# A graph layer's sum tiles in PSUM: zeroed by TensorE instead of ScalarE, and counts with a one-column weight

## The chip, the cores and the metric

The kernel runs on one core of one Trainium2 chip, in one launch. A time is the device time of one execution in microseconds. The kernel before has a median of 3023.34 us over 12 runs (3010.74 to 3027.88).

## The reference, cut to what matters

Two relational graph convolutions and a mixture of experts, on 6250 nodes with 256 features, 100000 edges sorted by target, 8 relations:

```python
def _rgcn_conv(x, W, Wroot, b, src, dst, etype):
    xs = x[src]
    seg = dst * R + etype                                   # R = 8
    sums = jax.ops.segment_sum(xs, seg, num_segments=N * R)
    cnt = jax.ops.segment_sum(jnp.ones_like(xs[:, 0]), seg, num_segments=N * R)
    mean = (sums / jnp.maximum(cnt, 1.0)[:, None]).reshape(N, R, -1)
    return x @ Wroot + b + jnp.einsum('nrd,rde->ne', mean, W)

h = relu(_rgcn_conv(layernorm(x), W1, Wroot1, b1, src, dst, edge_type))
x = x + _rgcn_conv(h, W2, Wroot2, b2, src, dst, edge_type)
x = x + ffn(layernorm(x))      # 8 experts, the best 2 of each row, gelu between two products
```

The change lies in the two segment sums (`sums` and `cnt`).

## The kernel before, in words

The program has four stages. The first normalises `x` and writes it to HBM as three bf16 parts (`xs`), since the sums are made of bf16 products of three parts each. It also works out each edge's place, and sets `flag`: 1 if the edges lie where a plan expects them (every edge in its window, every window in its bounds). If it is 1, the two graph layers run as function `layer` (k = 0 and 1); otherwise a generic arm does that work, with an edge list sorted by indirect DMAs. The last stage runs the experts; the change does not touch it.

**Tiles and groups.** The edges come in 782 tiles of 128. One to six consecutive tiles form a group, 194 groups in a layer, and a group's edges fall into a window of at most 64 consecutive target nodes (`WIN`). `_plan` fixes the groups, their windows' widths (`regions[r][5]`, `wd` in the code), the order in which two runs of groups, one upward and one downward through the nodes, are taken in turns (`seq`), and `whole[b]`, the step by which every edge into the 128-node block b has been added. `bounds` lists for each group which blocks its window may touch.

**A step.** `layer` runs through 194 steps (q). `tiles_in` of the next group takes a PSUM tile `pg` (two buffers), lets ScalarE fill it with zeros (L672), and for each tile of edges issues an indirect gather on GpSimd's queue (L680, the tile `ge`, 13 buffers) and one VectorE instruction that makes the one-hot matrix `oh` (L686). `sums` of this step's group multiplies each gathered tile with its `oh` on TensorE: six bf16 matmuls for two halves of the features and three parts (L696), and in layer 0 a seventh with a matrix of ones for the counts (L699). All of them add onto the zeros in PSUM. `add` adds `pg` to a ring in SBUF on VectorE (L710).

**Blocks.** Around it, by `whole[b]`: `root` loads a block's rows a step ahead; `counts` and `invert` give 1/count; `project`, two steps after `whole[b]`, multiplies the block's sums with the nine weight matrices (36 f32 matmuls, L783) and collects them on VectorE (L791, L793); `clear` zeroes the block's part of the ring on ScalarE (L800); `finish` and `turn` write the result and transpose it. All engines take their instructions in order. The order within a step is `tiles_in` of the next group, `project` and `clear`, `turn`, `finish`, `sums`, `invert`, `add`, `root` and `counts`. Layer 1's gathers read what layer 0's `finish` wrote, so layer 1 begins after layer 0's last block.

Because the group's adds and the block's matmuls touch the same ring, the program declares by `bounds` which of them need no order between them; `READ` and `TAKE` are the numbers of steps that these declarations allow.

Of the kernel before, what the change touches and what calls it, by code (L numbers as in the profile page):

```python
# [39 lines left out]
BF16 = mybir.dt.bfloat16  # L40
# [8 lines left out]
P = 128  # L49
# [45 lines left out]
Z = 4.8  # L95
WIN = 64
RB = 3
READ = 2
TAKE = 3
EARLY = 30  # L100

# [1 line left out]
def _plan(N, E, R):  # L103

    T = -(-E // P)

    def windows(ts, n):

        mid = n // 2
        lo, hi = [0] * n, [-(1 << 30)] * n
        for t in ts:
            for k in range(n + 1):
                i0, i1 = t * P, max(0, t + k - mid) * P
                mean = N * (i1 * i1 - i0 * i0) / (E * E)
                sd = 2 * N * i0 / (E * E) * math.sqrt(abs(i1 - i0)) + 0.004 * abs(mean)
                if k < n:
                    lo[k] = min(lo[k] if t != ts[0] else 1 << 30, math.floor(mean - Z * sd) - (k < mid))
                if k:  # L120
                    hi[k - 1] = max(hi[k - 1], math.ceil(mean + Z * sd) + (1 if k <= mid else 2))
        shift = -min(lo)
        w = [(a + shift, b + shift) for a, b in zip(lo, hi)]
        return shift, w, max(b for _, b in w)


    NB = -(-N // P)
    mid = max(0, round((N / 4 - P / 2) / P))
    split = round(T * math.sqrt((mid + 0.5) * P / N))
    regions = []  # L130
    t = 0
    while t < T:
        left = (split if t < split else T) - t
        for n in range(min(6, left), 0, -1):
            ng = max(1, min(36, left) // n)
            shift, w, width = windows((t + n // 2, t + n * (ng - 1) + n // 2), n)
            if width <= WIN:
                break
        regions.append((t, n, ng, shift, w, width))
        t += n * ng  # L140
    groups = []
    for r, (t0, n, ng, *_) in enumerate(regions):
        for g in range(ng):
            groups.append((t0 + g * n, n, r))
    NG = len(groups)
    up = [g for g in range(NG) if groups[g][0] < split]
    down = list(range(NG - 1, len(up) - 1, -1))
    size = [sum(groups[g][1] for g in s) for s in (up, down)]
    seq, at, n = [], [0, 0], [0, 0]
    while len(seq) < NG:  # L150

        s = int(n[1] * (size[0] - EARLY) < n[0] * size[1])
        if at[s] == len((up, down)[s]):
            s = 1 - s
        g = (up, down)[s][at[s]]
        seq.append(g)
        at[s] += 1
        n[s] += groups[g][1]
    step = {g: q for q, g in enumerate(seq)}

    whole = []
    for b in range(NB):
        if b == mid:
            whole.append(NG - 1)
            continue
        p = math.sqrt((b + 1 if b < mid else b) * P / N)
        dev = Z * math.sqrt(E * p * (1 - p)) + 1
        t = int(min(E - 1, E * p + dev) // P) if b < mid else int((E * p - dev) // P)
        whole.append(step[next(g for g, (t0, n, _) in enumerate(groups) if t0 + n > t)])


    bounds = []
    for g in range(NG):
        read, taken = ([b for b in range(NB) if whole[b] + n < step[g]] for n in (READ - 1, TAKE))
        if g < len(up):
            bounds.append((sum(b < mid for b in read) or -NB, sum(b < mid for b in taken) + RB))
        else:
            n = sum(b > mid for b in read)
            bounds.append((NB - sum(b > mid for b in taken) - RB, NB - n if n else 2 * NB))
    return T, regions, groups, seq, len(up), mid, whole, bounds  # L180
# [3 lines left out]
def kernel(  # L184
# [20 lines left out]
    nc = tc.nc  # L205
    N, D = x.shape
    E = src.shape[0]
    R = gW1.shape[0]
    X = fW1.shape[0]
    H = fW1.shape[2]  # L210
    KD = D // P
    KH = H // P
    NB = -(-N // P)
# [20 lines left out]
    def rows(i):  # L234
        return P if i < NB - 1 else LAST
# [6 lines left out]
    ones16 = const.tile([P, P], BF16, name="ones16")  # L242
# [82 lines left out]


    T, regions, groups, seq, UP, mid, whole, bounds = _plan(N, E, R)
    assert T == C
    NG = len(groups)
# [306 lines left out]
    with tc.If(go == 1) as cmp:  # L636
        with ExitStack() as arm:
            TR = MM = 2
            TT = "mm"
            ap = arm.enter_context(tc.tile_pool(name="ap", bufs=2, side="right"))  # L640
            invs = ap.tile([P, NB, R], F32, name="invs", bufs=1)
            hTs = ap.tile([P, NB, KD, P], F32, name="hTs", bufs=1)
            zeros = ap.tile([P, WIN], F32, name="zeros", bufs=1)
            nc.vector.memset(zeros, 0.0)
            rings = [ap.tile([P, KD + 1, R, RING + WIN], F32, name=f"ring{i}", bufs=1) for i in range(2)]

            step = {g: q for q, g in enumerate(seq)}
# [8 lines left out]
            def layer(k):  # L656
                nd = KD + 1 if k == 0 else KD
# [8 lines left out]
                state = {}  # L666

                def tiles_in(g):
                    t0, n, r = groups[g]
                    pg = psum.tile([P, nd, R, WIN], F32, name="pg", tag="pg", bufs=2)  # L670
                    wd = regions[r][5]
                    state["zeroed"] = nc.scalar.copy(pg[:, :nd, :, :wd],  # L672
                                                     zeros[:, None, None, :wd].to_broadcast([P, nd, R, wd]))
                    got = []
                    ohs = ap.tile([P, OHW], BF16, name="oh", bufs=3)
                    o0 = 0
                    for t in range(t0, t0 + n):
                        m = P if t < EC else ER
                        ge = ap.tile([P, 3, KD, P], BF16, name="ge", bufs=13)
                        nc.gpsimd.indirect_dma_start(  # L680
                            out=ge[:m].rearrange("p s k d -> p (s k d)"), out_offset=None, in_=xs[k][:, :],
                            in_offset=bass.IndirectOffsetOnAxis(ap=idx[:m, t : t + 1], axis=0))
                        a, b = regions[r][4][t - t0]
                        oh = ohs[:m, o0 : o0 + (b - a) * R].rearrange("p (r d) -> p r d", r=R)
                        o0 += (b - a) * R
                        nc.vector.tensor_scalar(oh, iota16[:m].rearrange("p (r d) -> p r d", r=R)[:, :, a:b],  # L686
                                                rel[:m, t : t + 1], None, op0=OP.is_equal)
                        got.append((ge, oh, m, a, b))
                    state[g] = (pg, got)

                def sums(g):
                    pg, got = state[g]
                    for ge, oh, m, a, b in got:
                        for c in range(KD):
                            for s in range(3):
                                nc.tensor.matmul(pg[:, c, :, a:b], ge[:m, s, c, :], oh, start=False, stop=False,  # L696
                                                 skip_group_check=True)
                        if nd > KD:
                            nc.tensor.matmul(pg[:, KD, :, a:b], ones16[:m], oh, start=False, stop=False,  # L699
                                             skip_group_check=True)  # L700

                def add(g):
# [132 lines left out]
                def logits(b):  # L835
                    if k == 1:
                        gate(place[b], state.pop(("t", b)), rows(b))
                        for o, bs in batches[:-1]:
                            if b == bs[-1]:
# [3 lines left out]
                                todo.extend((j, i, False, c) for j, i in enumerate(bs))  # L843

                tiles_in(seq[0])
                due = {}
                for b, q in enumerate(whole):
# [45 lines left out]
    with cmp.Else():  # L893
        with ExitStack() as arm:
# [35 lines left out]
            with tc.tile_pool(name="sortp", bufs=1, side="right") as sp:  # L930
# [22 lines left out]
                for d in range(NB):  # L953
                    oh = sp.tile([P, C], F32, name="oh", bufs=2)
# [16 lines left out]
                for d in range(NB):  # L971
                    oh = sp.tile([P, C], F32, name="oh", bufs=2)
# [11 lines left out]
                for j in range(C):  # L984
                    n = P if j < EC else ER
# [11 lines left out]
                for i in range(NB):  # L997
                    n = rows(i)
# [13 lines left out]
                for j in range(C):  # L1012
                    a = sp.tile([P, P], F16, name="ca", bufs=4)
                    nc.vector.tensor_scalar(a, iota_k[:, :P], df[:, j : j + 1], None, op0=OP.is_equal)
                    b = sp.tile([P, NK], F16, name="cb", bufs=4)
# [7 lines left out]
            ap = lay.enter_context(tc.tile_pool(name="aggp", bufs=2, side="right"))  # L1023
# [65 lines left out]
            for i in range(NB):  # L1089
                n = rows(i)  # L1090
# [10 lines left out]
            with tc.tile_pool(name="ggate", bufs=2) as gp, tc.If(go == 0):  # L1101
                for o, bs in batches:
                    for j, i in enumerate(bs):
                        n = rows(i)
# [5 lines left out]
                    if i != order[-1]:  # L1110
                        c = choose(bs, o, gp, "mm", MM)
# [162 lines left out]
```

## Time and profile before

| | |
|---|---|
| median of 12 runs | 3023.34 us |
| the profiled execution | 3020.25 us, of which its span is 3018.4 us |
| busy over the span | TensorE matmul 2557.0 us, weight loads 2158.7, GpSimd 1808.6, VectorE 1621.7, ScalarE 1018.8 |
| gathers of edges (L680) | 1564, 1519.7 us, the first at 83.8 and the last at 2153.4 us |
| sums (L696) and counts (L699) | 9384 and 782 matmuls, 837.4 and 189.0 us |
| block products (L783, from the ring) | 3072 matmuls of 128x256 f32, 727.2 us |
| zeroing of `pg` (L672) | 388 copies on ScalarE, 380.1 us |
| adding to the ring (L710) | 388 on VectorE, 456.5 us |

In the profile an instruction is named by its line, its engine and the tile that it writes and reads (`pg<-oh,ge`). PE is TensorE's matmul, PEld its weight load, DVE is VectorE, ACT ScalarE, POOL GpSimd. What stands behind an arrow `<-` after an idle time is what ended that idle time. A matmul's busy time includes the end of its pipeline, so a busy engine can still start matmuls closer together.

### The profile page before, as it was taken

To read this page: it belongs to the slowest core of one execution; us is meant where nothing else is said; L and a number is where in the kernel's file an instruction comes from. 1 tells how busy PE (TensorE), PEld (TensorE's weight loads), DVE (VectorE), ACT (ScalarE), POOL (GpSimd) and SP (SyncE) were. 2 spreads that over 40 slices of the span, in tenths; PEclk is the share of its full clock that TensorE was granted. 3 is DMA by queue.
4 is the path that set the end of the run, shared out by engine and by line. 5 is a ranking of instruction groups with operands and counts; after the bars stand their busy time and mean duration, and the time that the engine had idled before them with its cause. 6 is when DMAs were issued, how large, how long until landed. Compare 5 with 4: busy or idle time off the path is not lost.

```text
span 3018.4 us, 52037 instructions
## 1 busy us (share of the span) xinstructions
PE 2557.0 (85%) x18131; PEld 2158.7 (72%) x18131; DVE 1621.7 (54%) x4676; ACT 1018.8 (34%) x1378; POOL 1808.6 (60%) x2109
## 2 busy tenths in 40 slices
PE   5578887888888886887888888898839999999997
PEld 2467776776777765666766776777628888888886
DVE  7567676766676674666766776676711111111111
ACT  6434444434344342332323322232312222222221
POOL 1667777777777765777777777777413333333332
PEclk9689999999999997988989998899969999999999
DMA  7555565655565544666566666666363444444441
GB/s 248 157 151 164 168 172 165 172 158 169 161 174 165 166 140 140 178 176 174 170 173 176 173 176 172 173 183 174 108 200 114 116 111 107 108 122 107 107 121 20
DMA packets 215591, 461.05 MB, mean 153 GB/s; under 512 B 50716, under 2 KB 123222, under 8 KB 215190
## 3 DMA queue, kind: packets, MB, share of 16 engines
q0 software_dynamic: 120384, 334.45, 41.2%
q1 hardware_dynamic: 83724, 112.33, 11.1%
q10 hardware_dynamic: 11210, 10.81, 1.1%
q8 instruction: 149, 2.44, 0.3%
q14 instruction: 124, 1.02, 0.1%
HBM read 412.02 MB, written 46.31 MB: 152 GB/s over the span
## 4 chain that ended last, share of the span: by engine, by line
PE 63%; DMA 20%; ACT 5%; issue 5%; DVE 4%; POOL 2%; SPq 0%; DVEq 0%; ACTq 0%; POOLq 0%
PE pr L783 25%; DMA ge<-xs,idx 15%; PE ph L1214 12%; PE po L1225 12%; PE pg L696 10%; ACT ring L800 2%; DVE ring L710 2%; POOL ge L680 2%; DMA xt<-in_x_dram 2%; ACT pg L672 2%; DMA cn<-ring 1%; PE pt L1198 1%; PE pg L699 1%; DMA fw<-in_L_ffn_W_dram 1%; PE pt L314 1%
## 5 line engine op out<-in xcount | busy, mean ns | idle before, releaser
L680 POOL DMA_INDIRECT ge<-xs,idx x1564 | 1519.7, 972 | 617.1 <-issue 215.0
L696 PE MATMUL pg<-oh,ge 128*128 128x200 bf16 (+24 forms) x9384 | 837.4, 242 | 314.4 <-DMA ge<-xs,idx 220.7
L696 PEld LDWEIGHTS <-ge 128*128 128x128 bf16 x9384 | 675.5, 105 | 439.4 <-DMA ge<-xs,idx 280.3
L783 PE MATMUL pr<-gw,ring 128*128 128x256 f32 (+1 forms) x3136 | 744.1, 392 | 1.1 <-DVE h L793 0.6
L783 PEld LDWEIGHTS pr<-gw,ring 128*128 128x128 f32 (+1 forms) x3136 | 609.6, 197 | 95.3 <-DVE h L793 5.0
L710 DVE TENSOR_TENSOR ring<-pg,ring 128x1176 f32 (+31 forms) x388 | 456.5, 1176 | 285.8 <-PE pg L696 145.3
L672 ACT COPY pg<-zeros 128x1176 f32<-128x1176 f32 (+31 forms) x388 | 380.1, 981 | 543.8 <-DVE ring L710 500.3
L793 DVE SCALAR_TENSOR_TENSOR h<-pr,invs,h 128x256 f32<-128x256 f32 (+1 forms) x784 | 376.5, 480 | 159.3 <-PE pr L783 142.1
L800 ACT COPY ring<-zeros 128x3072 f32<-128x3072 f32 (+1 forms) x98 | 227.8, 2324 | 670.4 <-PE pr L783 610.3
L1215 ACT ACTIVATE hT<-ph,bcol 128x256 f32<-128x256 f32 x424 | 200.3, 473 | 535.9 <-PE ph L1214 535.9
L1214 PE MATMUL ph<-xT,w 128*128 128x256 f32 x1696 | 379.6, 383 | 0.0
L1225 PE MATMUL po<-fw,hT 128*128 x1696 | 374.4, 379 | 0.0
L1225 PEld LDWEIGHTS po<-fw,hT 128*128 128x128 f32 x1696 | 322.2, 190 | 43.8
L1214 PEld LDWEIGHTS ph<-xT,w 128*128 128x128 f32 x1696 | 322.0, 192 | 42.6
L686 DVE TENSOR_SCALAR oh<-iota,rel 128x152 bf16<-128x152 f16 (+25 forms) x1564 | 336.8, 274 | 19.0 <-PE pg L699 14.1
L1186 POOL DMA_INDIRECT xg<-xnd,ti x106 | 105.3, 994 | 348.9 <-DMA ti<-tlist 250.4
L1230 POOL DMA_INDIRECT out_dram<-fo,ti x106 | 168.6, 1591 | 231.5 <-DVE wt L1199 119.1
L1228 DVE TENSOR_TENSOR fo<-po,b2b 128x256 f32<-128x256 f32 x106 | 45.0, 424 | 299.5 <-PE po L1225 299.5
L699 PE MATMUL pg<-oh,ones 128*128 128x128 bf16 (+24 forms) x782 | 189.0, 242 | 0.0
L1209 DVE COPY bcol<-b1c 128x8 f32 x53 | 9.4, 179 | 302.1 <-ACT hT L1215 301.6
L699 PEld LDWEIGHTS <-ones 128*128 128x128 bf16 x782 | 83.0, 106 | 2.7
L783 PE MATMUL pr<-gw,hTs 128*128 128x256 f32 (+1 forms) x196 | 70.6, 483 | 2.3 <-ACT hTs L831 2.1
(190 smaller groups left out, 1344.9 us busy)
## 6 DMA issues: line engine op xcount, KB each, us to landing
w<-in_L_ffn_W_dram SPq DMA_DIRECT2D x53, 1024.0 KB
ge<-xs,idx POOLq DMA_INDIRECT x1564
xt<-in_x_dram SPq DMA_DIRECT2D x96, 128.0 KB
xs<-xb SPq DMA_DIRECT2D x8, 1152.0 KB
xs<-hb SPq DMA_DIRECT2D x48, 192.0 KB
fw<-in_L_ffn_W_dram ACTq DMA_DIRECT2D x8, 1024.0 KB
xt<-in_x_dram SPq DMA_DIRECT2D x8, 768.0 KB
out_dram<-h SPq DMA_DIRECT2D x48, 128.0 KB
```

Of the source, the lines that this page charges most:

```text
L672: state["zeroed"] = nc.scalar.copy(pg[:, :nd, :, :wd], zeros[:, None, None, :wd].to_broadcast([P, nd, R, wd]))
L680: nc.gpsimd.indirect_dma_start(out=ge[:m].rearrange("p s k d -> p (s k d)"), out_offset=None, in_=xs[k][:, :], in_offset=bass.IndirectOffs ...
L686: nc.vector.tensor_scalar(oh, iota16[:m].rearrange("p (r d) -> p r d", r=R)[:, :, a:b], rel[:m, t : t + 1], None, op0=OP.is_equal)
L696: nc.tensor.matmul(pg[:, c, :, a:b], ge[:m, s, c, :], oh, start=False, stop=False, skip_group_check=True)
L699: nc.tensor.matmul(pg[:, KD, :, a:b], ones16[:m], oh, start=False, stop=False, skip_group_check=True)
L710: a = nc.vector.tensor_tensor(slot, pg[:, :nd, :, :wd], slot, OP.add).ins
L783: mm = nc.tensor.matmul(pr[:n, j], chunks[c], w[:, c, r, :], start=(c == 0), stop=(c == KD - 1))
L793: nc.vector.scalar_tensor_tensor(h[:n], pr[:n, j], invs[:n, b, r : r + 1], h[:n], op0=OP.mult, op1=OP.add)
L800: ins = nc.scalar.copy(at, zeros[:, None, None, 0:1].to_broadcast([P, nd, R, P]))
L1214: nc.tensor.matmul(ph[:, :TK], w1[:, k, h * P : (h + 1) * P], xT[:, k, :], start=(k == 0), stop=(k == KD - 1))
L1215: nc.scalar.activation(hT[:, h, :], ph[:, :TK], AF.Gelu, bias=bcol[:, h : h + 1], scale=1.0)
L1225: nc.tensor.matmul(po[:, :D], hT[:, k, f * P : (f + 1) * P], rhs, start=(k == 0), stop=(k == KH - 1))
```

## The change

For all but the first three steps of a layer, ScalarE's copy of zeros into `pg` is gone. Instead `sums` begins with one matmul for each feature half (and in layer 0 one for the counts) that multiplies a bf16 matrix of ones with a bf16 tile of zeros, of the window's width times 8 relations, and that starts the accumulation. The zeros' tile is filled once by VectorE. The counts' matmul takes one column of the ones instead of 128 and writes one partition of `pg` instead of 128; only that partition is read from the ring. In `_plan` the margin of `whole` grows from 1 edge to 32 (a quarter of a tile), and the lower bound of a group's window counts a block as read as soon as its `whole` step is past, instead of one step later.

```diff
-READ = 2
...
-        dev = Z * math.sqrt(E * p * (1 - p)) + 1
+        dev = Z * math.sqrt(E * p * (1 - p)) + P / 4
...
-        read, taken = ([b for b in range(NB) if whole[b] + n < step[g]] for n in (READ - 1, TAKE))
+        read, taken = ([b for b in range(NB) if whole[b] + n < step[g]] for n in (0, TAKE))
...
+            zeros16 = ap.tile([P, R * WIN], BF16, name="zeros16", bufs=1)
+            nc.vector.memset(zeros16, 0.0)
...
-                    state["zeroed"] = nc.scalar.copy(pg[:, :nd, :, :wd],
-                                                     zeros[:, None, None, :wd].to_broadcast([P, nd, R, wd]))
+                    if step[g] < 3:
+                        state["zeroed"] = nc.scalar.copy(pg[:, :nd, :, :wd],
+                                                         zeros[:, None, None, :wd].to_broadcast([P, nd, R, wd]))
...
                 def sums(g):
                     pg, got = state[g]
+                    wd = regions[groups[g][2]][5]
+                    for c in range(nd if step[g] >= 3 else 0):
+                        nc.tensor.matmul(pg[:, c, :, :wd], ones16, zeros16[:, : R * wd].rearrange("p (r d) -> p r d", r=R),
+                                         start=True, stop=False, skip_group_check=True)
...
-                            nc.tensor.matmul(pg[:, KD, :, a:b], ones16[:m], oh, start=False, stop=False,
+                            nc.tensor.matmul(pg[0:1, KD, :, a:b], ones16[:m, 0:1], oh, start=False, stop=False,
                                              skip_group_check=True)
```

## The prediction

> **What bounds the kernel now.** I cut the span into its stages first (busy time of each engine in a stretch: time, PE, PEld, DVE, ACT, POOL, then the granted TensorE clock as a share of full speed, the DMA share and GB/s):
>
> ```profile
> 84.00:1118.00 1034.00, 856.31 (x7333) 733.26 (x7334) 704.49 (x1659) 436.73 (x476) 765.15 (x782) 0.92 0.57 164
> 1118.00:1156.00 38.00, 26.91 (x155) 21.93 (x153) 21.43 (x49) 12.74 (x17) 0.83 (x1) 0.85 0.13 41
> 1156.00:2154.00 998.00, 834.80 (x6721) 690.86 (x6722) 668.47 (x2178) 301.81 (x363) 753.18 (x782) 0.91 0.62 175
> 2154.00:2205.00 51.00, 29.52 (x179) 23.14 (x178) 30.19 (x124) 13.51 (x17) 0.38 (x1) 0.81 0.09 26
> 2205.00:3018.40 813.40, 764.22 (x3614) 669.94 (x3613) 142.14 (x446) 201.60 (x425) 273.98 (x212) 0.97 0.43 114
> ```
>
> Only rows 1 to 4 hold `pg`: layer 0's gathers, its end, layer 1's gathers, its end. In them TensorE is busiest, at 83% and 84%, GpSimd 74% and 75%; that seems to name TensorE. The timeline of GpSimd says otherwise:
>
> ```profile
> 603.13 0.94 POOL L680 DMA_INDIRECT ge<-xs,idx  x1 [0.30 <-issue]
> 604.37 0.94 POOL L680 DMA_INDIRECT ge<-xs,idx  x1 [0.30 <-issue]
> 605.62 0.94 POOL L680 DMA_INDIRECT ge<-xs,idx  x1 [0.30 <-DMA ge<-xs,idx]
> ```
>
> A gather takes 0.94 us and the next follows after 0.30 us whatever is named as the releaser, so the queue's own pace is 1.25 us. 782 x 1.25 = 978 us of layer 0's 1034 and of layer 1's 998. The rest: gathers longer than 0.946 us (765 - 740 = 25 us and 753 - 740 = 13 us), and waits for a free `ge` buffer, which the waits of layer 0's stretch give:
>
> ```profile
> POOL ge L680 <- PE pg L696: 79.8, 171, 5.9
> POOL ge L680 <- PE pg L699: 18.2, 49, 2.7
> ```
>
> 220 waits of 0.30 us are the pace itself (66 us); 98 - 66 = 32 us are real. Layer 1's corresponding row is 110.3 us over 340 waits: 8 us. 978 + 25 + 32 = 1035 and 978 + 13 + 8 = 999 close both stretches. **So GpSimd sets the pace, and TensorE enters the time through these 40 us and the two ends.** TensorE's own waits, layer 0 and then layer 1:
>
> ```profile
> PE pg L696 <- DMA ge<-xs,idx: 88.2, 101, 15.9
> PE pg L696 <- ACT pg L672: 70.7, 63, 4.4
> ```
>
> ```profile
> PE pg L696 <- DMA ge<-xs,idx: 132.5, 176, 5.1
> PE pg L696 <- ACT pg L672: 13.4, 16, 1.8
> ```
>
> The wait that the change removes is 84 us, but most of it lies behind the 1.25 us pace.
>
> **The change part by part.**
>
> *ScalarE loses* 382 of 388 copies, 382 x 0.981 = 375 us. It is no bound (42% and 30% busy). What counts is the 84 us for which TensorE waited; not all of it goes, since the new matmul also waits for the ring add two steps back (the second `pg` buffer). ScalarE's row has that chain: its zeroing idles 500.3 us for DVE's L710. Where the add itself was late, the wait stays; I keep 16% and take 70 us as removed, 59 in layer 0 and 11 in layer 1.
>
> *TensorE gains* 191 x 3 matmuls in layer 0 and 191 x 2 in layer 1, 955 in all. Evaluating the plan's widths, the 191 groups have 75,472 columns, 395 each. No row has that shape. Bound it by starts of neighbouring bf16 matmuls in the timeline:
>
> ```profile
> 255.88 0.71 PE L696 MATMUL pg<-oh,ge 128*128 128x200 bf16 x6
> 256.42 0.26 PE L699 MATMUL pg<-oh,ones 128*128 128x200 bf16 x1
> 256.51 0.71 PE L696 MATMUL pg<-oh,ge 128*128 128x200 bf16 x6
> ...
> 259.88 0.44 PE L830 MATMUL pt<-ident,h 128*128 128x128 f32 x2 [1.94 <-DVE h L808]
> ...
> 260.91 1.20 PE L696 MATMUL pg<-oh,ge 128*128 128x200 bf16 x6 [0.25 <-ACT pg L672]
> ```
>
> Seven of 200 columns in 0.63 us are 90 ns each; the same at 72 columns (617.10 to 617.36 us) gives 37. The slope, 0.414 ns a column, gives 90 + 195 x 0.414 = 171 ns; in proportion it would be 178; the f32 product of 256 columns, 209 ns (956 in 200 us), is the upper end. I take 171, the nearest rows' line. At the granted 0.92 and 0.91: 573 x 171 / 0.92 = 107 us and 382 x 171 / 0.91 = 72 us, that is 0.56 and 0.38 us a step. Behind the new wait stands the whole of TensorE's queue for that step; before, the same queue stood behind ScalarE's copy.
>
> *Layer 0, first half (84 to 600 us).* 106 steps x 0.56 = 59 us in, 51.6 us of ACT waits there, of which I count 43 as gone: +16. TensorE waits for gathers 40.0 us there, 15.9 of it once; 24 are cover, but in the stretches with real buffer waits there is none. I take a third of the 16 as reaching GpSimd: +5.
> *Second half (600 to 1118).* 83 steps x 0.56 = 47 us in, 16 of 19.1 out: +31, under 48.2 us of gather waits. What shows are the buffer waits after two block products close together, 38.3 + 8.2 - 106 x 0.30 = 15 us in a few places; one or two steps' zeros make each later by about 1 us: +3.
> *Layer 1.* 72 in, 11 out, under 132.5 us of cover; its 8 us of buffer waits grow by about 1.
> *The ends.* After the last gather TensorE works off what is left; five copies on ScalarE start after 1098 us, 2.4 us as matmuls, and TensorE waits 1.90 + 0.53 us for them now: 0.
>
> *Counts.* 782 loads of one column instead of 128. The 128-column load takes 0.10 us but lies under the running matmul: the six matmuls before the ones' take 0.54 us (255.88 to 256.42), the ones' itself 0.09, so it costs what the others do. So 0; were a load exposed, 782 x 0.1 = 78 us, but no row shows that, and I keep +-8 us (10 ns each). The Trainium skill ("TensorE: Matmul & The Clock Gate", Weight-path perf modes) speaks against this edit: the fast weight load applies only to 128 weights that are not FP32, so a one-column load loses it. By that page's own P/1.2 rule one column is still under a nanosecond and the sum would stay.
>
> *The plan.* Evaluated with both margins, two of 49 blocks move one step later (block 17 from 164 to 165, block 44 from 28 to 29), with their `counts`, `project`, `clear`, `finish` and the DMAs of these on SP's queue; neither is the last, so 0. For the reference's inputs every window stays at least 11 rows inside its new bounds, so `flag` stays 1. The zeros' memset: a memset of 128x1536 on DVE took 1.34 us (L739), a third of the elements 0.45, ahead of the first gather at worst.
>
> Sum: 5 + 3 + 1 = +9 us on the profiled 3020.25, that is 3029; this execution lay 3.1 us under the median, so the prediction on the median is 3032.
>
> **The clock** is the main uncertainty. After the 1.94 us idle at 257.9 the same six matmuls take 1.20 instead of 0.71 us, and the granted clock is 0.54 from 260.0 to 263.6 us after 1.00 before; between 628 and 639 us, with gathers awaited 0.64 to 1.23 us at a time, it is 0.54 too. So thin work halves the clock here, and zeros put work into such idle time. The skill's page just named (Why this matters for your kernels) puts the limit at idle gaps of over about 3 us; by it the gaps above would have been harmless and the zeros would gain nothing. The rows decide: shorter gaps do it.
>
> **The rivals.**
> *Faster: the clock and the removed waits win.* Layers 0 and 1 run at 0.92 and 0.91; at 0.96 the 856 + 835 us of TensorE work would shrink by some 4%, 70 us, as much as half of what the zeros add, and the block products that now run at half speed and cause the buffer waits would be short. At best all 40 us of buffer waits go, 2980; half of them, 3003. It decides if the granted clock in the layers rises above about 0.95. For it: the first half's longest idle times are those behind ACT. Against it: GpSimd's pace leaves only these 40 us to gain.
> *No change.* All zeros fall into gather waits: 88 + 132 us of cover against 179 - 70 = 109. Then 3020 to 3028. Against it: little cover where the buffer waits are.
> *Clearly slower: TensorE becomes the bound in layer 0.* 856 + 107 + the other waits (about 28 us) + 12 that remain = 1003 us, equal to GpSimd's 978 + 25. Two chains of equal length with 13 buffers between them wait for each other; if of the 107 - 59 = 48 us net half is not covered, +24 in layer 0 and +3 in layer 1: 3050.
> *It does not do what it says:* a window outside its bounds sends everything to the generic arm, whose 782 scatters to the edge list alone are 978 us at the gathers' pace: above 4000 us. 1 in 100.
>
> **How the numbers follow.** About 0.2%, 6 us, is what a measurement here can tell from no change. Slower by more: the forecast 30 in 100, the bound 12, the generic arm 1: 0.43. Within: 0.29. Faster: 0.28. The range goes from 3003 (half the buffer waits gone) to 3050.
>
> **What would show it.** Right: gathers still 1.25 us apart; L672 with 6 copies; new rows on PE with `pg<-zeros,ones`, 955 of them, near 171 ns apart at full clock; PE's waits for ACT's L672 gone, for DVE's L710 new but below 20 us; GpSimd's real buffer waits between 40 and 60 us. Wrong: those waits below 25 us with a clock above 0.95 (the faster rival), or above 70 us, or a changed gather pace.

## The result, and the profile after

The changed kernel takes 3051.28 us (median of 11 runs, 3040.79 to 3057.32), the kernel before beside it 3021.64 us: a ratio of 1.0096 [1.0085, 1.0107], slower by 30 us; 9 us more were forecast (3032 us on the earlier median of 3023.34), with a range from 3003 to 3050 us. The profiled execution took 3052.47 us, of which 3050.7 are its span. The four experiments `e5_counts_64`, `e6_counts_65`, `e7_counts_last` and `e8_no_zeroing` shared a chip on which the kernel before itself took 3832.38 us and engines waited up to 23 us at a time for something that the profile gives no cause for (VectorE's ring add in `e8_no_zeroing`), so their times say something only beside that one.

The profile after, cut into the same stages (time, PE, PEld, DVE, ACT, POOL, granted clock, DMA share, GB/s):

```profile
82.00:1149.00 1067.00, 1022.95 (x7878) 755.49 (x7888) 705.93 (x1663) 232.59 (x287) 769.15 (x782) 0.97 0.56 159
1149.00:1188.00 39.00, 29.46 (x175) 22.62 (x173) 21.92 (x50) 12.57 (x16) 0.68 (x2) 0.92 0.12 38
1188.00:2192.00 1004.00, 871.57 (x7114) 711.18 (x7121) 679.43 (x2184) 148.54 (x174) 755.10 (x782) 0.94 0.61 175
2192.00:2240.00 48.00, 26.14 (x163) 20.22 (x161) 28.00 (x121) 12.21 (x16) 0.22 (x1) 0.79 0.09 27
2240.00:3050.70 810.70, 762.83 (x3614) 669.08 (x3613) 141.26 (x443) 202.00 (x425) 274.49 (x212) 0.97 0.44 115
```

Against the rows of before the stretch of layer 0's gathers grew from 1034 to 1067 us, layer 1's from 998 to 1004; the other stages changed by -3 to +1 us each. So the loss is in layer 0's gather stretch. TensorE is busy there for 1023 us instead of 856, although its granted clock rose from 0.92 to 0.97. Two rows of TensorE's waits in this stretch, and two of GpSimd's (for a free `ge` buffer), show who waits for whom now:

```profile
PE pg L702 <- DMA ge<-xs,idx: 30.8, 16, 16.0
PE pg L697 <- DVE ring L716: 11.5, 10, 1.7
```

```profile
POOL ge L682 <- PE pg L702: 116.9, 204, 6.6
POOL ge L682 <- PE pg L705: 18.7, 46, 2.0
```

TensorE's 1023 us of work and these 42 us of waits are 1065 of the stretch's 1067 us: it is idle for hardly anything else. The wait for ScalarE's zeros (70.7 us before) is gone. Of GpSimd's 250 waits 250 x 0.30 = 75 us are its own pace, and 135.6 - 75 = 60 us are real, 32 before. With the pace and the longer gathers that accounts for the stretch as it did before: 978 + 29 + 60 = 1067.

Where TensorE's new work is, the timeline shows at the place that the prediction used (start, busy, and in brackets the idle time before):

```profile
256.75 0.68 PE L697 MATMUL pg<-zeros,ones 128*128 128x392 bf16 x3 [1.21 <-DVE ring L716]
257.27 0.70 PE L702 MATMUL pg<-oh,ge 128*128 128x200 bf16 x6
257.91 0.25 PE L705 MATMUL pg<-oh,ones 128*1 128x200 bf16 x1
258.09 0.71 PE L702 MATMUL pg<-oh,ge 128*128 128x200 bf16 x6
258.74 0.25 PE L705 MATMUL pg<-oh,ones 128*1 128x200 bf16 x1
```

Three zero matmuls take 0.52 us (256.75 to 257.27), 173 ns each. The six sums and the counts of one tile take 0.82 us from start to start (257.27 to 258.09), where before seven took 0.63. Five spaces of 90 ns after the first sum put the last sum at 257.72; the counts follow 0.19 us later and the next sum 0.18 us after that, instead of 0.09 and 0.09. **So the one-column matmul holds up TensorE on both sides, by some 95 ns each.** Over all pairs the median spacings in ns are:

| columns of the moving operand | 72 | 112 | 152 | 200 | 272 |
|---|---|---|---|---|---|
| sum to sum, before and after; and sum to counts before | 37 | 50 (53 after) | 70 | 90 | 116 |
| sum to one-column counts | 139 | 143 | 166 | 186 | 209 |
| one-column counts to what follows | 130 | 143 | 163 | 183 | 210 |

The weight load itself is no dearer. The groups of the page (times, busy us, mean ns, and the idle time before them with what ended most of it):

```profile
L697 PE MATMUL pg<-zeros,ones 128*128 128x392 bf16 (+16 forms) x939 | 235.7, 341 | 13.1 <-DVE ring L716 12.2
L705 PE MATMUL pg<-oh,ones 128*1 128x128 bf16 (+24 forms) x782 | 177.4, 227 | 0.0
L705 PEld LDWEIGHTS <-ones 128*1 128x1 bf16 x782 | 61.9, 79 | 99.4 <-issue 51.8
```

A load of one column takes 79 ns, shorter than the 101 ns of the sums' loads in the same profile. What grew is the time around it: 2 x 95 ns x 782 = 149 us of TensorE's time if every tile followed closely on the one before.

### The profile page after: what moved, and what is told of

It reads as the page before. It is cut to its first block, busy times and chain, and to the rows that moved or that the text cites. A ratio compares the mean times of both kernels' runs of the same rounds, so it can differ in the third digit from the quotient of the medians.

```text
span 3050.7 us, 53428 instructions
## 1 busy us (share of the span) xinstructions
PE 2757.0 (90%) x19070; PEld 2197.9 (72%) x19086; DVE 1630.8 (53%) x4677; ACT 659.6 (22%) x996; POOL 1814.6 (59%) x2110
## 5 line engine op out<-in xcount | busy, mean ns | idle before, releaser
L702 PE MATMUL pg<-oh,ge 128*128 128x200 bf16 (+24 forms) x9384 | 850.5, 235 | 160.6 <-DMA ge<-xs,idx 153.8
L702 PEld LDWEIGHTS <-ge 128*128 128x128 bf16 x9384 | 631.6, 101 | 315.2 <-DMA ge<-xs,idx 182.9
L789 PE MATMUL pr<-gw,ring 128*128 128x256 f32 (+1 forms) x3136 | 736.7, 388 | 1.7 <-DVE h L799 1.5
L789 PEld LDWEIGHTS pr<-gw,ring 128*128 128x128 f32 (+1 forms) x3136 | 601.5, 195 | 95.1 <-DVE h L799 6.7
L697 PE MATMUL pg<-zeros,ones 128*128 128x392 bf16 (+16 forms) x939 | 235.7, 341 | 13.1 <-DVE ring L716 12.2
L705 PE MATMUL pg<-oh,ones 128*1 128x128 bf16 (+24 forms) x782 | 177.4, 227 | 0.0
L705 PEld LDWEIGHTS <-ones 128*1 128x1 bf16 x782 | 61.9, 79 | 99.4 <-issue 51.8
```

The source lines that it names most:

```text
L697: nc.tensor.matmul(pg[:, c, :, :wd], ones16, zeros16[:, : R * wd].rearrange("p (r d) -> p r d", r=R), start=True, stop=False, skip_group_c ...
L705: nc.tensor.matmul(pg[0:1, KD, :, a:b], ones16[:m, 0:1], oh, start=False, stop=False, skip_group_check=True)
L789: mm = nc.tensor.matmul(pr[:n, j], chunks[c], w[:, c, r, :], start=(c == 0), stop=(c == KD - 1))
```

## The experiments

Theory A: the one-column counts cost the time, by holding up TensorE at each change of the weight's width, and layer 0 pays as soon as TensorE's work no longer fits behind GpSimd's pace. Rival B: the zero matmuls cost it. Rival C: the plan's change does. In the expectations, which are printed as they were written, A is called S and later M, B is Z and C is P; theory G there says that GpSimd's 1.25 us a gather sets the time, and "drain" means the delay beside a narrow matmul. The first three kernels take the parts one by one.

**Zeros and plan alone** (`e1_zero_only`: the changed kernel with 128-column counts).

```diff
-    nc.tensor.matmul(pg[0:1, KD, :, a:b], ones16[:m, 0:1], oh, ...)
+    nc.tensor.matmul(pg[:, KD, :, a:b], ones16[:m], oh, ...)
```

> The kernel after, but its counts load 128 columns of ones as before (zeroing on TensorE and the plan's margins stay). Theory S (the one-column load interrupts TensorE's stream): the trace of the change shows 186 ns from the last sum to the ones' matmul at 200 columns and 183 ns from it to the next, 90 and 90 before, so 190 ns x 782 = 149 us of TensorE time in layer 0; without it the time is 3016 to 3030 us, ratio 0.998 to 1.003, and GpSimd's real waits for a buffer in layer 0 fall to some 35 us. Theory Z (the 955 zeroing matmuls, 179 us, make TensorE the bound): 3045 to 3055 us, as the change. Theory P (the plan's margins): as the change too.

Measured: 3018.75 us, ratio 0.9976 [0.9964, 0.9988], just below the 0.998 expected. Its row of layer 0's gathers:

```profile
84.00:1116.00 1032.00, 910.96 (x7881) 763.45 (x7891) 702.79 (x1658) 230.42 (x285) 769.84 (x782) 0.95 0.57 165
```

The zeros with the plan are a gain of 7 us. By an estimate, the 856 us of TensorE's work at a clock of 0.918 would be 824 at this run's 0.954 (the rows' 0.92 and 0.95 to three digits), so the higher clock alone would return 32 of the 573 x 170 ns / 0.954 = 102 us that the zeros take. That makes 926 us; measured are 911, and the other 15 us are not accounted for. That the zeros raise the clock shows in two kernels below, which differ from this one in zeros alone: 0.91 without any, 0.98 with twice as many.

**Counts alone** (`e2_counts_only`: the kernel before with the counts' edit).

```diff
-    nc.tensor.matmul(pg[:, KD, :, a:b], ones16[:m], oh, ...)
+    nc.tensor.matmul(pg[0:1, KD, :, a:b], ones16[:m, 0:1], oh, ...)
```

> The kernel before, and only its counts load one column of ones and write one partition. Theory S: 149 us more TensorE time in layer 0 beside the copies on ScalarE, which still make TensorE wait: 3045 to 3060 us, layer 1 unchanged within 3 us. Theory Z or P: 3021 us within 6, since the loads lie under running matmuls.

Measured: 3054.01 us, ratio 1.0100 [1.0084, 1.0115], as much as the whole change costs. Layer 1, which has no counts, takes 1003 us for its gathers, 5 more than before where at most 3 were expected. Its row of layer 0's gathers and GpSimd's waits there:

```profile
82.00:1150.00 1068.00, 968.75 (x7339) 724.51 (x7340) 708.46 (x1663) 441.16 (x478) 764.45 (x782) 0.93 0.55 159
```

```profile
POOL ge L680 <- PE pg L696: 120.1, 210, 6.3
POOL ge L680 <- PE pg L699: 30.1, 69, 3.8
```

The stretch is the changed kernel's to a microsecond, and its real buffer waits are 150.2 - 279 x 0.30 = 66 us. The number of TensorE's instructions is that of before; only 782 of them became narrower.

**The plan alone** (`e3_plan_only`).

```diff
-        dev = Z * math.sqrt(E * p * (1 - p)) + 1
+        dev = Z * math.sqrt(E * p * (1 - p)) + P / 4
...
-        read, taken = (... for n in (READ - 1, TAKE))
+        read, taken = (... for n in (0, TAKE))
```

> The kernel before with only the plan's change (margin of 32 edges, a block counts as read at its whole step): two blocks move by one step. Theories S and Z: 3021 us within 5. Theory P: 3040 us or more.

Measured: 3019.71 us, ratio 0.9986 [0.9978, 0.9995]. Rival C is out; if anything the plan is 4 us to the good, and no row of its profile shows where (both gather stretches are as long as before, 1034 and 998 us).

**How narrow must it be?** `e4_counts_100`, `e6_counts_65` and `e5_counts_64` are the kernel before with counts of 100, 65 and 64 columns.

```diff
-    nc.tensor.matmul(pg[:, KD, :, a:b], ones16[:m], oh, ...)
+    nc.tensor.matmul(pg[0:64, KD, :, a:b], ones16[:m, 0:64], oh, ...)
```

> The kernel before, with counts that load 100 columns of ones and write 100 partitions. It tells apart why the one-column load interrupts the stream. If what counts is that a load has fewer than the full 128 columns: 95 ns on either side of each counts matmul as with one column, and the time of e2. If what counts is that only one column, or only the first 32-wide part of the array, is used: starts 90 ns apart at 200 columns and 3021 us within 6.

> The kernel before, with counts of 65 columns, one more than half the array. Theory M: no change of tiling, 90 ns between starts at 200 columns, 3021 us within 6. Rival (the stall grows gradually as the load gets narrower): between 3022 and 3055 us, starts between 90 and 186 ns apart.

> The kernel before, with counts that load 64 columns of ones and write 64 partitions. The 100-column counts cost nothing (starts 90 ns apart at 200 columns), the one-column counts 95 ns on either side. Theory M (the array changes its column tiling for a stationary operand of at most 64 columns, and drains on each change): as with one column, some 186 and 183 ns at 200 columns, 149 us more TensorE time and 3045 to 3060 us. Rival (only a very narrow load, or a load that takes no time under the running matmul, does it): 90 ns and 3021 us within 6.

Measured: 3024.68 us, ratio 0.9994 [0.9983, 1.0005], for 100 columns; 3830.18 us, 1.0002 [0.9987, 1.0016], for 65; 3836.65 us, 0.9999 [0.9975, 1.0023], for 64. With 100 columns the load's own row rises from 101 to 128 ns (medians), yet at 200 moving columns the counts and the sum behind them still follow after 90 ns each. So a load of fewer than 128 columns, the prediction's own objection to this edit, can be dearer and stays hidden; it is not the cause. TensorE's timeline of the 65-column kernel, then of the 64-column one:

```profile
278.14 0.26 PE L699 MATMUL pg<-oh,ones 128*65 128x200 bf16 x1
278.23 0.71 PE L696 MATMUL pg<-oh,ge 128*128 128x200 bf16 x6
278.77 0.26 PE L699 MATMUL pg<-oh,ones 128*65 128x200 bf16 x1
278.86 0.71 PE L696 MATMUL pg<-oh,ge 128*128 128x200 bf16 x6
```

```profile
276.82 0.28 PE L699 MATMUL pg<-oh,ones 128*64 128x200 bf16 x1
277.03 0.71 PE L696 MATMUL pg<-oh,ge 128*128 128x200 bf16 x6
277.67 0.28 PE L699 MATMUL pg<-oh,ones 128*64 128x200 bf16 x1
277.88 0.71 PE L696 MATMUL pg<-oh,ge 128*128 128x200 bf16 x6
```

At 65 columns a tile takes 0.63 us (278.23 to 278.86) and the sum follows the counts after 0.09; at 64 it takes 0.85 us (277.03 to 277.88), with 0.21 after the counts. One column more or less, and the delay is there or not. It is therefore a switch, not a load that becomes dearer column by column. On this chip the 64-column kernel's time did not move, against the 3045 to 3060 us expected. GpSimd's real waits for a buffer in layer 0 are 447.8 - 224 x 0.30 = 381 us there with 64 columns and 422.7 - 184 x 0.30 = 367 us with 65, against 32 in the profile of before; why the delays don't show in the time beside that is open. So this pair shows the spacing and not the time.

The Trainium skill has a rule for this ("TensorEngine Tiling (Array Packing)", Key Properties): changing the tiling mode, as opposed to the tile, drains TensorE; under Performance Considerations it gives 64 columns or fewer of the stationary operand as the case for column tiling. The step between 65 and 64 columns is where these two sentences would put it. That the narrow counts change the mode is inferred from this, as no row of a trace names a mode. The runs put the price at some 95 ns on either side.

**One run of counts for each group** (`e7_counts_last`, and on another chip `e7b_counts_last`: the changed kernel, with the counts of all tiles of a group behind the sums of all of them). If the change of width costs and not the narrow matmul, a group pays once.

```diff
     for ge, oh, m, a, b in got:
         ...
-        if nd > KD:
-            nc.tensor.matmul(pg[0:1, KD, :, a:b], ones16[:m, 0:1], oh, ...)
+    for ge, oh, m, a, b in got if nd > KD else []:
+        nc.tensor.matmul(pg[0:1, KD, :, a:b], ones16[:m, 0:1], oh, ...)
```

> The kernel after (zeros on TensorE, one-column counts), but a group's counts are issued behind one another after its sums. Theory M: the stream is interrupted once a group, not once a tile, 194 x 190 ns = 37 us in place of 149 us, and within a run of counts they follow at the plain 90 ns; 3018 to 3030 us. Rival (each one-column load stalls by itself, whatever stands before it): as the change, 3045 us or more.

> The kernel after, with a group's one-column counts behind one another after its sums. Theory M (a drain on each change of the array's column tiling): 194 x 190 ns = 37 us of TensorE time instead of 149; where before takes some 3022 us, 3018 to 3032 us. Rival (each one-column load stalls by itself): 3045 us or more.

Measured: 3852.27 us, ratio 1.0054 [1.0034, 1.0075], and on the other chip 3020.74 us, 1.0000 [0.9990, 1.0009]. TensorE's timeline of the second:

```profile
203.09 1.25 PE L702 MATMUL pg<-oh,ge 128*128 128x200 bf16 x12
204.26 0.34 PE L705 MATMUL pg<-oh,ones 128*1 128x200 bf16 x2
204.54 0.68 PE L697 MATMUL pg<-zeros,ones 128*128 128x392 bf16 x3
```

Twelve sums, 11 x 90 ns, end their starts at 204.08; the first count comes 0.18 us later, the second 0.09 after it, the zeros 0.19 after that. The matmuls are as many and as narrow as in the changed kernel; with the delay paid once a group instead of once a tile, the loss of 30 us is gone. The chip of the first run lost 0.5% by this order, and why is open.

**No zeroing at all** (`e8_no_zeroing`, and on another chip `e8b_no_zeroing`). As in `e1_zero_only`, but the zero matmuls are gone, and the first product into each bank of `pg` begins its accumulation. It often covers only a part of its group's columns (200 of 392, by the zeros and sums of the changed kernel's timeline); nothing else clears the others, and they too begin from zero, since the sums come out right.

```diff
-    for c in range(nd if step[g] >= 3 else 0):
-        nc.tensor.matmul(pg[:, c, :, :wd], ones16, zeros16[...], start=True, ...)
...
-    nc.tensor.matmul(pg[:, c, :, a:b], ge[:m, s, c, :], oh, start=False, ...)
+    nc.tensor.matmul(pg[:, c, :, a:b], ge[:m, s, c, :], oh, start=ge is got[0][0] and s == 0, ...)
...
-    nc.tensor.matmul(pg[:, KD, :, a:b], ones16[:m], oh, start=False, ...)
+    nc.tensor.matmul(pg[:, KD, :, a:b], ones16[:m], oh, start=ge is got[0][0], ...)
```

> The kernel after with 128-column counts and without any zeroing from the fourth step on: the first sums matmul of a group into each bank of the tile starts the accumulation, and a column that no matmul has written since is overwritten by the first that reaches it; the windows of a group's tiles cover its whole width. The step takes 179 us from TensorE against e1, and no ScalarE copy comes back. Theory G (GpSimd's 1.25 us per gather sets the pace, TensorE enters only through waits for a free gather buffer): 3003 to 3018 us, at best some 30 us below before, and real buffer waits in layer 0 below 25 us. Rival (TensorE's work is the bound of layer 0): some 100 us of it come off, 2930 to 2990 us.

> The kernel after with 128-column counts and no zeroing from the fourth step on: the first sums matmul of a group into each bank of the tile starts the accumulation, and a column not written since is overwritten by the first matmul that reaches it. Against the kernel with zeros on TensorE alone (0.9976 of before) 179 us of TensorE work go. Theory G (GpSimd's 1.25 us a gather sets the pace): ratio 0.991 to 0.998 where before takes some 3022 us. Rival (TensorE's work is the bound of layer 0): 0.97 or less.

Measured: 3811.10 us, ratio 0.9952 [0.9933, 0.9970], and 3008.13 us, 0.9954 [0.9940, 0.9967]: **13 us faster than before on the second chip, the best version here** (the plan's change is part of it). Layer 0's gathers:

```profile
83.00:1099.00 1016.00, 861.25 (x7336) 737.32 (x7337) 697.70 (x1663) 231.25 (x287) 759.96 (x782) 0.91 0.58 168
```

**Twice the zeros** (`e9_zeros_twice`: `e1_zero_only`, with each zero matmul issued two times).

```diff
-    for c in range(nd if step[g] >= 3 else 0):
+    for c in list(range(nd if step[g] >= 3 else 0)) * 2:
```

> The kernel with zeros on TensorE and 128-column counts, and every zeroing matmul issued twice: 107 us more TensorE work in layer 0 and 72 in layer 1. Theory G (what counts is TensorE's total in layer 0 against GpSimd's 1003 us, whatever it is made of): layer 0's stretch grows by some 15 to 25 us, layer 1's by under 8; 3030 to 3050 us. Rival (zeroing matmuls are hidden wherever they stand, only the drains cost): 3015 to 3025 us.

Measured: 3021.96 us, ratio 1.0001 [0.9990, 1.0013].

```profile
82.00:1116.00 1034.00, 973.73 (x8452) 806.30 (x8452) 708.40 (x1663) 231.65 (x286) 762.82 (x782) 0.98 0.57 165
```

Even doubled, the zeros leave the stretch at 1034 us; the clock is 0.98. Rival B is out as the cause of the loss; beside no zeroing at all, on the same chip, the doubled zeros cost 14 us. Theory G's own expectation, a stretch longer by 15 to 25 us and 3030 us or more, missed here, and its rival's 3015 to 3025 us came.

**One-column counts without the sums' zeros** (`e10_counts_no_zeroing`: `e8_no_zeroing` with one-column counts; only the counts' bank still has its zero matmul; the lines are against the changed kernel).

```diff
-    for c in range(nd if step[g] >= 3 else 0):
-        nc.tensor.matmul(pg[:, c, :, :wd], ones16, zeros16[...], start=True, ...)
+    if nd > KD and step[g] >= 3:
+        nc.tensor.matmul(pg[:, KD, :, :wd], ones16, zeros16[...], start=True, ...)
...
+    nc.tensor.matmul(pg[:, c, :, a:b], ge[:m, s, c, :], oh, start=ge is got[0][0] and s == 0, ...)
```

> One-column counts, with only the counts' bank zeroed on TensorE (36 us in layer 0) and the sums' banks not zeroed at all: 149 us of drains and 36 us of zeros in layer 0 against 149 and 107 in the change, nothing in layer 1. Theory G: between e8b and the change, some 10 to 25 us below the change in layer 0: 3022 to 3042 us. Rival (the drains alone cost the change's 30 us, since they break the stream in the catching-up stretches): 3042 to 3053 us.

Measured: 3030.54 us, ratio 1.0033 [1.0019, 1.0048].

```profile
82.00:1128.00 1046.00, 978.49 (x7514) 729.31 (x7515) 703.76 (x1657) 232.51 (x286) 763.61 (x782) 0.95 0.57 163
```

Beside the best version on the same chip the narrow counts, with the one zero matmul a group that they still have, cost 22 us. This time theory G's range came, and not its rival's.

## Why the prediction was right or wrong

The table has layer 0's gather stretch for the runs on chips where the kernel before takes 3021 to 3026 us; `e3_plan_only` and `e4_counts_100` are left out, as they repeat the row of before (1034 and 1032 us). Load is TensorE's busy time and its waits at a group's start for a free `pg`, be it for ScalarE's zeros or for VectorE's add to have read it; the last column adds GpSimd's 978 us of pace, what its gathers took beyond 740, and the real buffer waits.

| kernel | stretch | clock | load | closes as |
|---|---|---|---|---|
| `e8b_no_zeroing` | 1016 | 0.91 | 861 + 38 = 899 | 978 + 20 + 18 |
| `e1_zero_only` | 1032 | 0.95 | 911 + 21 = 932 | 978 + 30 + 25 |
| before | 1034 | 0.92 | 856 + 71 = 927 | 978 + 25 + 32 |
| `e7b_counts_last` | 1037 | 0.96 | 942 + 17 = 959 | 978 + 26 + 33 |
| `e9_zeros_twice` | 1034 | 0.98 | 974 + 9 = 983 | 978 + 23 + 33 |
| `e10_counts_no_zeroing` | 1046 | 0.95 | 978 + 20 = 998 | 978 + 24 + 45 |
| `e2_counts_only` | 1068 | 0.93 | 969 + 40 = 1009 | 978 + 24 + 66 |
| after | 1067 | 0.97 | 1023 + 11 = 1034 | 978 + 29 + 60 |

**What bounds the kernel: right for the kernel before, no longer so for the changed one.** GpSimd's pace of 1.25 us is in every run (median 1.251 us, 1.254 after). That the three terms add up to every stretch within 1 us proves little: they only list what GpSimd's time went into, and would add up whichever engine held it up. What shows the bound is how the stretch reacts. From `e1_zero_only` to `e9_zeros_twice` TensorE's busy time grows by 63 us and the stretch by 2. Up to a load of 983 us the real buffer waits stay between 18 and 33 us; from 998 us on they are 45 to 66. The prediction put GpSimd's own time at 978 + 25 = 1003 us, and that is about where the loads begin to show. In the changed kernel TensorE's work and waits fill 1065 of the 1067 us, and GpSimd waits for it.

**The step that failed is "Counts".** The prediction set the one-column load at 0 ±8 us, because the weight load lies under the running matmul. That much holds (the load took 79 ns, though, not the part of a nanosecond that the prediction worked out), but the load was not the cost. The step looked at a width only through its load and never asked what a change of width does to the matmuls on both sides. The price stood in the trace of the kernel before, in layer 1, where 98 matmuls with 8 weight columns (`rpl`, 128 moving columns) lie among other work; TensorE's timeline there:

```profile
1280.17 0.22 PE L411 MATMUL rpl<-rcol,rnum 128*8 128x128 bf16 x1
1280.32 0.26 PE L696 MATMUL pg<-oh,ge 128*128 128x200 bf16 x1
1280.51 0.22 PE L411 MATMUL rpl<-rcol,rnum 128*8 128x128 bf16 x1
1280.66 0.44 PE L696 MATMUL pg<-oh,ge 128*128 128x200 bf16 x3
```

The narrow matmul starts 0.19 us after a sum of 200 columns, where another sum would start after 0.09; the sum behind it starts 0.15 us after it, where a second `rpl` behind a first starts after 0.056 (median of 25 pairs). That is the same 95 ns or so on each side, and 782 x 190 ns from this row would have given the term's size. The term measures 782 x 190 ns = 149 us of TensorE's time at full clock where all is close together; in busy time it is 969 - 856 = 112 us in `e2_counts_only`, less, I think, because a tile that is followed by a wait for a gather hides the second half. In the kernel's time it is +30 us alone (ratio 1.0100) and 1.0096 / 0.9976, some +36 us, beside the zeros, with the two ratios from two comparisons.

**The zeros: size right, effect put too high.** 171 ns was taken, 170 measured for the 392-column form, at full clock. The prediction let 5 + 3 + 1 us of them through; measured with the plan it is -7 us, of which the plan alone has -4, and doubled 0; the zeros' own -3 us are within the two intervals. Its removed waits for ScalarE came as said (70.7 us to none, the new wait for VectorE's add 11.5 us, below its 20). What it undersized is the clock: it charged the zeros at 0.92, and the clock of layer 0 rose to 0.95 with them and 0.98 with twice as many. Its reading of the clock needs a word: of the waits for gathers that it places between 628 and 639 us, those of 0.98 to 1.23 us lie between 621 and 627 us, where the clock was still 1.00; inside its stretch they are at most 0.79 us.

**The faster rival** named its condition, a clock above 0.95. It came, but real buffer waits fell only from 32 to 25 us in `e1_zero_only`. (Its 70 us are 39% of the zeros' 179, not half.) What the rival hoped for came in part without any zeros: `e8b_no_zeroing` has the old clock and 18 us of waits, so here it was the lighter load and not the clock.

**"TensorE becomes the bound in layer 0" happened, by another load.** The rival filled layer 0 with zeros to 1003 us and gave 3050 us; with the zeros alone the load is 932 us. The narrow counts brought it to 1034. The number is near the measured one, but the rival's reason is not the cause.

**The signs set beforehand** read so: gathers 1.25 us apart, the six copies of L674, 955 zero loads and the vanished wait for ScalarE, all as forecast; real buffer waits of 60 us, at the edge of the 40 to 60 that stood for the forecast. Layer 1, which has no counts, changed by 6 us where +1 was said, and by +1 to +8 in the other kernels of the table.

**The plan: 0 forecast, -4 us measured.** It is small, and its place isn't found.

**Left open.** `e9_zeros_twice` and `e10_counts_no_zeroing` have nearly equal busy times (974 and 978 us), yet differ by 12 us in the stretch. With the waits for `pg` their loads differ by 15 us, which would do. Where the work stands may count too: zeros stand at a group's start, where TensorE may wait for its first gather anyway, and the delays of the counts between tiles that have already come. No run separates the two. Load alone doesn't order everything either: `e2_counts_only` has a lower one than the changed kernel and 6 us more of buffer waits. The 7 us of `e1_zero_only` are not found in the gather stretches of its one profile either (-2 and +3 us).

## What to carry to other kernels

Don't narrow a matmul's weights to 64 columns or fewer between wide ones to save work: price the change of width on both neighbours, and if the narrow form is needed, run the narrow ones together. Before a form is priced by its neighbours, look for it in the whole trace, also in stages that the change doesn't touch. Where an engine hides behind another's pace, add up its load in that stretch against the pace first: here a load of 983 us in place of 927 left the stretch at 1034 us, and at 998 us and more it grew. A tile that is zeroed only so that products can add onto it needs no zeroing if the first product begins the accumulation.

## What the runs showed of the hardware

- Between 65 and 64 columns of weights a bf16 matmul among 128-column ones goes from no delay to some 95 ns before it and 95 to 120 ns after it; at 200 moving columns one weight column gives 186 and 183 ns from start to start, 64 columns 186 and 210, 65 and 100 columns 90 and 90 where nothing else is waited for. Narrow matmuls behind one another pay it once.
- Added products with zeros raise the granted clock of layer 0's gather stretch: 0.91 without, 0.95 with 573 of them, 0.98 with twice as many. The narrow counts alone gave 0.93, where the kernel before had 0.92.
- A weight load of fewer columns isn't always shorter: its row has a median of 101 ns with 128 columns, 128 with 100, 116 with 65, 106 with 64 and 79 with one.
- The first product into a bank also lets the columns that it does not write begin from zero: that made the zeroing needless. With the plan's change it gave 0.9954 [0.9940, 0.9967] of before, where zeros on TensorE gave 0.9976 [0.9964, 0.9988].
